# A graph layer with top-16 attention: two broadcasts, the output's products and the gates of the gathers are placed anew in a hand-written order

## The chip, the cores and the metric

One NeuronCore of one Trainium2 chip. The metric is the time of one execution in device microseconds.

## The reference

12500 nodes with 128 features, 200000 edges sorted by their target node. Cut to what matters:

```
h = relu(layernorm(x))
Qv = h @ W_Q.T ; Ku = h @ W_K.T
score = sum(Qv[dst] * Ku[src]) / sqrt(128) * exp(-edge_weight)
keep = the 16 highest scores of each dst
alpha = softmax of the kept scores within each dst
agg = segment_sum(alpha * (h[src] @ W_msg.T), dst)
out = x + relu(h @ W_self.T + agg)
```

## The kernel before

A beginning normalizes all rows of x into a table in memory (`h_tab`) and prepares the edges' tables; it takes the first 200 us or so. The rest is a software pipeline over 112 groups (`G`) of edges. A group is 14 chunks (`GC`) of 128 edges, and a fifteenth chunk (`NJ`) that overlaps the next group, so that every group holds whole nodes, at most 128 of them. Edges lie on the partitions, one chunk to a column.

One iteration of the loop over `i` is a pass. It works on several groups at once, each at another stage: `at(i - 3, sums, 0, 4)` runs the stage `sums` for group i − 3, if there is such a group. The order of the calls is the order on every engine: the schedule is manual, each engine runs its instructions in that order, and only semaphores join the engines.

The stages of a group g, by the pass in which they run:

- `h_turned`, `q_made`, `q_out` (passes g − 2 and g − 1): transpose the nodes' rows (TensorE), copy them out (`hT`), and multiply with the joint query and key weights, to `q`.
- `far_of(g, b)` and `to_edges(g, b)`, b from 0 to 3 (pass g − 1): TensorE copies the row of the edges' distances to the group's first node (`rel`) to all partitions, one bf16 product of up to 512 columns for four chunks (L223, a<-rel,ident), into one of two banks tagged "a". VectorE compares that with the partition's number (L631): `to_e`, a one-hot matrix from nodes to edges.
- `places(g)` (pass g − 1): VectorE builds the one-hot matrices of each edge's slot and of its node in a window (`opo`, L639 and L641).
- `q_to_edges(g, b)` (pass g): four fp32 products that give every edge its node's q, into one of two banks "q".
- `scores(g, b)` (pass g): VectorE multiplies the gathered source rows, the decay and q and sums along the row, once per chunk (L663). `scores_in_slots` spreads the scores over 40 slots (L671, L672).
- `slots_by_node`, `slots_out`, `node_by_slots` (pass g + 1): products that bring the scores of a node into one row.
- `best_begun`, `best`, `sum_of_exps`, `one_over_sum` (pass g + 2): the best 16 and their softmax.
- `kept_to_edges` (pass g + 2): 15 small bf16 products that bring each node's kept slots back to its edges, into bank "x" (L223, x<-km,to_e); `on_edges` (L732 to L739) and `exps` turn them into weights.
- `weights` (L747, L748), `sums`, `sums_out` (pass g + 3): one-hot matrices with weights, and 15 fp32 products that sum the gathered rows by node into bank "e"; ScalarE copies the sums out, divided by the softmax's sum (`agn`, L762).
- `sums_turned`, `sums_turned_out`, `products` (pass g + 4): transpose, copy (`aggT`, L769), and two fp32 products with the self and message weights.
- `output`, `store` (pass g + 5): relu and sum with x (L777), and the store.

One bank of PSUM, `so`, serves four of these: columns 0 to 127 the transposed rows, 128 to 255 the query product, 256 to 383 the transposed sums, 384 to 511 the output's products. VectorE's `output` reads it at the start of a pass, and `sums_turned` writes it right after.

The source rows come by an indirect DMA for each chunk, issued by GpSimd (L183), 14 in a pass, into one of 8 buffers, four to five groups ahead of their use. `gather_behind` makes each wait for the latest TensorE product issued before it in the order; `more(j)`, called 14 times in a pass, is such a gate. `PACED` is 12: until then the gathers run up to a third of a pass further ahead. `rows_asked`, `act_rows` and `rows_named` belong to other queues for single rows, whose rates (`SP_ROWS`, `ACT_ROWS`) are 0.

Of the kernel before, what the change touches and what calls it, by code (L numbers as in the profile page):

```python
# [19 lines left out]
ACT = mybir.EngineType.Activation  # L20

SP_ROWS = 0
ACT_ROWS = 0
PSUM = bass.MemoryType.PSUM

P = 128
# [57 lines left out]
def gnn_layer(  # L84
# [34 lines left out]
    G = -(-CH // GC)  # L119
# [20 lines left out]
    def bank(tag, bufs):  # L140
        return psum.tile([P, 512], F32, tag=tag, bufs=bufs, name=tag)
# [52 lines left out]
    for name, (_, _, p0, rate, j) in STREAMS.items():  # L194
        m = 0
        while rate:
            ready = p0 + (P * m + P - 1) // rate + 1
            g = max(ready, RAW)
# [29 lines left out]
    def gather_behind(g, j):  # L228

        if j < own[g] and (g, j) not in slow:  # L230
            d = gather(g, j, j + 1, lambda j: idx_all[:, GC * g + j:GC * g + j + 1])
            tc.add_manual_dep(d.ins, pe["last"].ins.name, SYNC, reason="behind a product")
# [41 lines left out]
    def raw_stats(g):  # L274
        T[g]["raw"] = row_stats(rows_pool, T[g]["hs"], own[g], f"r{g % 2}")
# [8 lines left out]
    def raw_finished(g, part):  # L284
        rows, (rs, sm) = T[g]["hs"], T[g]["raw"]
        if part < 3:
            normed(rows, 1 + 3 * part, 4 + 3 * part, rs, sm)
            return
        for t in range(10, own[g]):
            nc.vector.tensor_scalar(rows[:, t, :], rows[:, t, :], rs[:, t:t + 1], sm[:, t:t + 1],  # L290
                                    op0=OP.mult, op1=OP.add)
            nc.vector.tensor_scalar(rows[:, t, :], rows[:, t, :], 0.0, None, op0=OP.max)
# [18 lines left out]
    with tc.tile_pool(name="edges", bufs=1) as ep, ExitStack() as stage:  # L311
# [123 lines left out]
        pb = bank("s", 1)  # L435
# [79 lines left out]


    def all_checked():
        pb = bank("a", 2)
        nc.tensor.matmul(pb[0:1, 0:4], lhsT=ones, rhs=badc, start=True, stop=True)
        total = rows_pool.tile([1, 1], F32, name="total")  # L520
        nc.vector.tensor_reduce(total, pb[0:1, 0:4], axis=AX.X, op=OP.add)
        nc.vector.tensor_scalar(any_i, total, 1.0, None, op0=OP.min)
        nc.vector.tensor_scalar(uns, pb[0:1, 1:2], 1.0, None, op0=OP.min)
# [35 lines left out]
    with tc.tile_pool(name="win", bufs=2) as win:  # L559

        so = bank("s", 1)
# [29 lines left out]
        def load_x(g):  # L591
            k = G - TAIL
            if g == k:
                starts(g, 1, TAIL, XT)
            T[g]["x_t"] = rows_pool.tile([P, D], F32, name="x_t", bufs=8)
            if g < k:
                nc.sync.dma_start(T[g]["x_t"], x[ds(T[g]["start", 0], P), :])
            else:
                nc.sync.dma_start(T[g]["x_t"], x_end[ds(T[g]["start", 1], P), :])
# [193 lines left out]
        ready = {name: [] for name in STREAMS}  # L793
        unnamed = {name: [r for i in range(-3, G) for r in rows_at.get((name, i), [])] for name in STREAMS}

        def rows_named(name):

            todo = unnamed[name]
            g, j, e = todo[0]
            n = min(AT_ONCE, P - e)  # L800
            _, numbers = nc.values_load_multi_w_load_instructions(
                late_b[g:g + 1, j - GC + 2, e:e + n], engines=[STREAMS[name][1]], min_val=0, max_val=ROW * (N - 1),
                skip_runtime_bounds_check_because="nodes' numbers times a row's bytes")
            ready[name] += [(g, j, e + k, st) for k, st in enumerate(numbers)]
            del todo[:n]

        def rows_asked(name, most=1000):
            for g, j, e, st in ready[name][:most]:
                m = slow[g, j][1]
                if e == 0:  # L810
                    T[g]["late", j] = win.tile([P, D], F32, name=f"late{name}", bufs=NLATE)
                d = STREAMS[name][0].dma_start(T[g]["late", j][e:e + 1, :].bitcast(U8), h_bytes[ds(st, ROW)])
                d.then_inc(landed[name][m % NLATE], 16)
                tc.no_tile_sem_insts.add(d.ins.name)
                tc.add_to_no_dep_group(f"rows{g}_{j}", d.ins)
            del ready[name][:most]

        def act_rows(i, n):
            if i >= STREAMS["ACT"][2]:
                rows_asked("ACT", n)  # L820
# [6 lines left out]
        def at(g, stage, *args):  # L827
            if 0 <= g < G:
                stage(g, *args)


        for i in range(-3, G - 1):
            at(i + 3, load_nodes)
            due = len(rows_at.get(("SP", i), []))
            first = min(due, len(ready["SP"]))
            rows_asked("SP", first)
            at(i - 1, load_x)
            due -= first
            while due:
                rows_named("SP")  # L840
                n = min(due, len(ready["SP"]))
                rows_asked("SP", n)
                due -= n
            if i == G - 2:
                load_x(G - 2)
                load_x(G - 1)
            if i == 8:
                nc.sync.dma_start(h_tab[N:N + P, :], zpad)
                nc.sync.dma_start(x_end[XT:XT + P, :], zpad)
                nc.sync.dma_start(x_end[0:XT, :], x[N - XT:N, :])  # L850
            def raw(part):
                if i in (1, 2):
                    raw_finished(i + 1, part)

            def more(j):

                if i in (-1, 0, 1):
                    g = i + 6
                elif i < PACED:
                    g, j = (i + 4, j + 4) if j < 10 else (i + 5, j - 10)  # L860
                    if g < 8:
                        return
                else:
                    g = i + 4
                    if i == PACED and j < 4:
                        return
                if i >= -1 and g < G:
                    gather_behind(g, j)

            at(i, q_to_edges, 0)  # L870
            more(0)
            at(i - 5, output)
            at(i - 5, store)
            at(i - 4, sums_turned)
            at(i + 1, far_of, 0)
            at(i - 3, weights)
            at(i - 2, best_begun)
            at(i + 1, far_of, 1)
            more(1)
            at(i - 4, sums_turned_out)  # L880
            at(i + 1, q_out)
            act_rows(i, 3)
            at(i, q_to_edges, 1)
            more(2)
            raw(0)
            at(i + 1, to_edges, 0)
            at(i - 2, best)
            at(i - 2, sum_of_exps)
            act_rows(i, 4)
            for b in range(3):  # L890
                at(i - 1, slots_by_node, b)
            more(3)
            at(i + 1, to_edges, 1)
            at(i - 1, slots_out)
            at(i, scores, 0)
            raw(1)
            at(i + 1, far_of, 2)
            at(i + 1, far_of, 3)
            more(4)
            at(i, q_to_edges, 2)  # L900
            more(5)
            raw(2)
            at(i + 2, h_turned)
            at(i + 2, h_turned_out)
            at(i + 1, to_edges, 2)
            at(i, scores, 1)
            act_rows(i, 3)
            at(i - 2, kept_to_edges)
            more(6)
            at(i - 1, node_by_slots)  # L910
            at(i - 3, sums, 0, 4)
            more(7)
            at(i + 1, to_edges, 3)
            at(i - 3, sums, 4, 7)
            act_rows(i, 3)
            more(8)
            at(i, q_to_edges, 3)
            more(9)
            at(i - 2, one_over_sum)
            act_rows(i, 3)  # L920
            at(i - 3, sums, 7, 11)
            more(10)
            at(i - 3, sums, 11, NJ)
            more(11)
            at(i, scores, 2)
            at(i - 2, on_edges)
            at(i - 3, sums_out)
            at(i - 4, products)
            more(12)
            at(i - 2, exps)  # L930
            at(i + 1, places)
            if len(ready["ACT"]) < ACT_ROWS and unnamed["ACT"] and i >= 2:
                rows_named("ACT")
            act_rows(i, 4)
            at(i, scores, 3)
            at(i, scores_in_slots)
            if i == 0:
                raw_stats(2)
                raw_stats(3)
                raw_begun(2)  # L940
                raw_begun(3)
            if i in (1, 2):
                raw_finished(i + 1, 3)
            at(i + 2, q_made)
            more(13)
            if i > 0 and later:
                later.pop(0)()

# [95 lines left out]
    with tc.tile_pool(name="gen", bufs=1) as gen, tc.If(nc.values_load(  # L1044
# [31 lines left out]
        pb = bank("s", 1)  # L1076
# [142 lines left out]
```

## Time and profile before

| what | value |
|---|---|
| median of 3 runs | 2464.83 us (2458.7 to 2468.15) |
| the profiled execution | 2461.79 us, span 2460.0 us |
| TensorE matmuls, busy | 1633.1 us (66%), 13352 instructions |
| TensorE weight loads, busy | 1420.3 us (58%) |
| VectorE busy | 1668.7 us (68%), 7054 instructions |
| GpSimd busy | 1484.4 us (60%), of it gathers 1421.1 us in 1507 |
| ScalarE busy | 277.0 us (11%) |
| granted TensorE clock, mean | 0.806 |

In the rows of the order of time the first number is the start in us from the span's start, the second the length, then engine, line, operation, what is written and read, and in brackets the idle time of the engine before it and what ended that. "remote" is a release that the profile cannot name. A matmul's record shows when it was begun, and its end is modelled; one fp32 product of 128 by 128 is two records. L223 and L226 are the helpers that issue all products and transpositions of the loop, so there the tiles' names tell the stages apart.

### The profile page before, as it was taken

The page shows a single profiled execution, that of the slowest core. Times are in us where ns is not written, and L with a number is a line of the kernel's source. Part 1 is how long each engine was busy: PE and PEld are TensorE (multiplying, and loading weights), DVE is VectorE, ACT ScalarE, POOL GpSimd, SP SyncE. Part 2 cuts the span into 40 slices and gives each one's busy share as a digit, 9 for nine tenths or more (in the row PEclk, how much of TensorE's full clock was granted, in tenths as well). Part 3 has the DMA queues.
Part 4 walks back from the last instruction along what each step waited for, and adds up shares of the span by engine and source line. Part 5 has one row for each costly group of instructions (what it writes and reads, how often), then busy time and mean ns, then how long its engine had stood idle before and what let it go on. Part 6 is the DMA issues. An engine that isn't in the chain of part 4 may idle for free. (4 is left out here: it accounts for less than half of the span.)

```text
span 2460.0 us, 41443 instructions
## 1 busy us (share of the span) xinstructions
PE 1633.1 (66%) x13352; PEld 1420.3 (58%) x13353; DVE 1668.7 (68%) x7054; ACT 277.0 (11%) x1075; POOL 1484.4 (60%) x1579
## 2 busy tenths in 40 slices
PE   0337777766676676677676766767676767767676
PEld 0236666656565566666666655656565656656566
DVE  5557667666666666667666666666666666667676
ACT  5420000000000000001000000000000000001011
POOL 6653666666666666666666666666666666666640
PEclk9957788778777888787778788887888787888888
DMA  9311222222222222222222222222222222222210
GB/s 247 91 47 35 65 54 55 54 54 54 54 54 56 54 55 55 54 56 53 53 53 53 55 55 54 56 53 54 56 55 54 54 56 54 56 52 56 52 43 9
DMA packets 101470, 143.43 MB, mean 58 GB/s; under 512 B 31063, under 2 KB 74327, under 8 KB 100480
## 3 DMA queue, kind: packets, MB, share of 16 engines
q0 software_dynamic: 50144, 102.74, 16.5%
q1 hardware_dynamic: 51102, 37.99, 5.6%
q8 instruction: 106, 1.74, 0.3%
q14 instruction: 118, 0.97, 0.1%
HBM read 126.79 MB, written 14.40 MB: 57 GB/s over the span
## 5 line engine op out<-in xcount | busy, mean ns | idle before, releaser
L183 POOL DMA_INDIRECT hs<-h_tab,idx_all x1507 | 1421.1, 943 | 859.8 <-issue 308.0
L223 PEld LDWEIGHTS q<-q,to_e 128*128 128x128 f32 x3348 | 541.6, 238 | 255.2 <-DVE prod L663 201.2
L223 PE MATMUL q<-q,to_e 128*128 128x128 f32 x3348 | 589.5, 329 | 76.0 <-DVE prod L663 57.2
L631 DVE TENSOR_SCALAR to_e<-a,nvec 128x512 f32<-128x512 f32 (+1 forms) x447 | 318.8, 714 | 378.0 <-remote 239.6
L663 DVE SCALAR_TENSOR_TENSOR prod<-hs,dec_all,q 128x128 f32<-128x128 f32 x1674 | 482.5, 343 | 30.9 <-issue 15.9
L223 PE MATMUL e<-hs,alz 128*128 128x128 f32 x3240 | 477.1, 303 | 30.5 <-issue 30.2
L223 PEld LDWEIGHTS e<-hs,alz 128*128 128x128 f32 x3240 | 439.0, 215 | 34.6 <-issue 25.5
L226 PE MATMUL s<-ident,agn 128*128 128x128 f32 x112 | 41.6, 371 | 389.8 <-issue 225.8
L223 PE MATMUL e<-opo,sl 128*41 128x40 f32 x3348 | 233.0, 240 | 93.3 <-issue 93.2
L223 PEld LDWEIGHTS e<-opo,sl 128*41 128x41 f32 x3348 | 204.4, 155 | 127.8 <-issue 115.0
L226 PEld LDWEIGHTS s<-ident,agn 128*128 128x128 f32 x112 | 17.9, 160 | 407.6 <-issue 397.4
L223 PE MATMUL a<-rel,ident 112*128 112x512 bf16 (+1 forms) x447 | 185.3, 479 | 92.6 <-DVE km L709 68.9
L777 DVE SCALAR_TENSOR_TENSOR o<-s,x_t 128x128 f32<-128x128 f32 x112 | 32.6, 291 | 231.4 <-remote 223.4
L641 DVE TENSOR_TENSOR opo<-slots,x 128x1200 f32<-128x1200 f32 x109 | 153.0, 1404 | 3.8
L663 DVE DVE_READ_ACCUMULATOR prod<-hs,dec_all,q 128x1 f32 x1674 | 138.9, 83 | 0.1
L762 ACT ACTIVATE agn<-e,rden 128x128 f32<-128x128 f32 x108 | 39.7, 367 | 840.9 <-PE q L223 580.4
L769 ACT COPY aggT<-s 128x128 f32<-128x128 f32 x112 | 29.7, 265 | 607.6 <-remote 360.0
L748 DVE TENSOR_TENSOR alz<-opo,x 128x600 f32<-128x600 f32 x112 | 87.0, 777 | 3.9
L739 DVE TENSOR_REDUCE kept<-mine 128x15 f32<-128x600 f32 x112 | 86.9, 776 | 3.8
L672 DVE TENSOR_TENSOR sl<-opo,x 128x600 f32<-128x600 f32 x110 | 85.6, 778 | 3.8
L737 DVE TENSOR_TENSOR mine<-x,opo 128x600 f32<-128x600 f32 x112 | 86.5, 772 | 0.0
L223 PEld LDWEIGHTS <-to_e 128*128 128x128 bf16 x1674 | 74.7, 110 | 16.6 <-issue 9.1
(184 smaller groups left out, 1356.0 us busy)
## 6 DMA issues: line engine op xcount, KB each, us to landing
hs<-h_tab,idx_all POOLq DMA_INDIRECT x1507
h_r<-h_tab SPq DMA_DIRECT2D x112, 64.0 KB
x_t<-in_x_dram SPq DMA_DIRECT2D x108, 64.0 KB
out_dram<-o SPq DMA_DIRECT2D x108, 64.0 KB
xg<-in_x_dram SPq DMA_DIRECT2D x2, 1400.0 KB
h_tab<-xg SPq DMA_DIRECT2D x2, 1400.0 KB
xg<-in_x_dram SPq DMA_DIRECT2D x1, 1120.0 KB
h_tab<-xg SPq DMA_DIRECT2D x1, 1120.0 KB
```

What stands on the lines that cost most here:

```text
L183: d = nc.gpsimd.indirect_dma_start(out=T[g]["hs"][:, j, :], out_offset=None, in_=table[0:N, :], in_offset=bass.IndirectOffsetOnAxis(ap=ind ...
L223: pe["last"] = nc.tensor.matmul(*args, **how)
L226: pe["last"] = nc.tensor.transpose(*args)
L631: nc.vector.tensor_scalar(T[g]["to_e"][:, n0:n1], T[g]["pr", b][:, 0:n1 - n0], nvec, None, op0=OP.is_equal)
L641: nc.vector.tensor_tensor(T[g]["opo"], slots.unsqueeze(1).unsqueeze(1).to_broadcast([P, 2, NJ, KM]), at_e.unsqueeze(3).to_broadcast([P, 2, ...
L663: nc.vector.scalar_tensor_tensor(prod, rows_of(g, j), dec_all[:, c:c + 1], T[g]["pq", b][:, (j % 4) * P:(j % 4 + 1) * P], op0=OP.mult, op1 ...
L672: nc.vector.tensor_tensor(sl1[g % 2][:, 0:n, 0:KM], T[g]["po"][:, 0:n, :], bc(s[:, 0:n], KM), op=OP.mult)
L737: nc.vector.tensor_tensor(mine[:, 0:n, :], px[:, 0:n, 0:KM], T[g]["po"][:, 0:n, :], op=OP.mult)
L739: nc.vector.tensor_reduce(kept[:, 0:n], mine[:, 0:n, :], axis=AX.X, op=OP.add)
L748: nc.vector.tensor_tensor(alz[g % 2].rearrange("e (j w) -> e j w", w=WW + STEP)[:, 0:n, 0:WN], T[g]["ow"][:, 0:n, :], bc(kept[:, 0:n], WN) ...
L762: nc.scalar.activation(T[g]["agn"], T[g]["pa"], AF.Copy, scale=T[g]["rden"])
L777: nc.vector.scalar_tensor_tensor(T[g]["o"], so[:, 3 * P:4 * P], 0.0, T[g]["x_t"], op0=OP.max, op1=OP.add)
```

## The change

Two of the four broadcasts of distances (`far_of`, b 0 and 1) move from the start of the pass to the end of the pass before; they are then called for group i + 2. The output's two products (`products`) move from the end of a pass to its middle, behind broadcasts 2 and 3. The kept slots' products (`kept_to_edges`) move ahead of the third block of `q_to_edges`. `sums_out`, `places` and `q_made` come right behind scores block 2, and `on_edges` behind `places`. The 14 gates lie elsewhere between these steps. The gathers of groups 5, 6 and 7 run in passes 0, 1 and 2, where they ran in passes −1, 0 and 1. The calls of the row queue with rate 0 are taken out. The check of the edges' form, which runs once, uses bank `so` where it used a bank "a".

```diff
     def all_checked():
-        pb = bank("a", 2)
+        pb = so[:, 3 * P:4 * P]
...
-                if i in (-1, 0, 1):
-                    g = i + 6
+                if i in (0, 1, 2):
+                    g = i + 5
...
-                if i >= -1 and g < G:
+                if i >= 0 and g < G:
                     gather_behind(g, j)
 
             at(i, q_to_edges, 0)
...
             at(i - 5, output)
             at(i - 5, store)
             at(i - 4, sums_turned)
-            at(i + 1, far_of, 0)
             at(i - 3, weights)
             at(i - 2, best_begun)
-            at(i + 1, far_of, 1)
             more(1)
...
             at(i + 1, far_of, 2)
             at(i + 1, far_of, 3)
             more(4)
-            at(i, q_to_edges, 2)
+            at(i - 4, products)
+            at(i - 2, kept_to_edges)
             more(5)
             raw(2)
+            at(i, q_to_edges, 2)
+            more(6)
             at(i + 2, h_turned)
             at(i + 2, h_turned_out)
             at(i + 1, to_edges, 2)
             at(i, scores, 1)
-            act_rows(i, 3)
-            at(i - 2, kept_to_edges)
-            more(6)
             at(i - 1, node_by_slots)
...
             at(i, scores, 2)
+            at(i - 3, sums_out)
+            at(i + 1, places)
+            at(i + 2, q_made)
+            more(12)
+            at(i + 2, far_of, 0)
+            at(i + 2, far_of, 1)
+            more(13)
             at(i - 2, on_edges)
-            at(i - 3, sums_out)
-            at(i - 4, products)
-            more(12)
             at(i - 2, exps)
-            at(i + 1, places)
...
             at(i, scores, 3)
             at(i, scores_in_slots)
...
-            at(i + 2, q_made)
-            more(13)
```

More of the change, by code (lines that the diff above doesn't have):

```diff
@@ L888, in gnn_layer @@
             at(i - 2, sum_of_exps)
-            act_rows(i, 4)
             for b in range(3):
@@ L906, in gnn_layer @@
             at(i, scores, 1)
-            act_rows(i, 3)
-            at(i - 2, kept_to_edges)
-            more(6)
             at(i - 1, node_by_slots)
@@ L914, in gnn_layer @@
             at(i - 3, sums, 4, 7)
-            act_rows(i, 3)
             more(8)
@@ L919, in gnn_layer @@
             at(i - 2, one_over_sum)
-            act_rows(i, 3)
             at(i - 3, sums, 7, 11)
@@ L925, in gnn_layer @@
             at(i, scores, 2)
+            at(i - 3, sums_out)
[5 more added lines that the diff above has]
+            more(13)
             at(i - 2, on_edges)
-            at(i - 3, sums_out)
-            at(i - 4, products)
-            more(12)
             at(i - 2, exps)
-            at(i + 1, places)
-            if len(ready["ACT"]) < ACT_ROWS and unnamed["ACT"] and i >= 2:
-                rows_named("ACT")
-            act_rows(i, 4)
             at(i, scores, 3)
```

## The prediction

> **What bounds the kernel now.** I read the page first, then the stretches by pass, then the waits, then the order of time around one pass boundary.
>
> ```profile
> span 2460.0 us, 41443 instructions
> PE 1633.1 (66%) x13352; PEld 1420.3 (58%) x13353; DVE 1668.7 (68%) x7054; ACT 277.0 (11%) x1075; POOL 1484.4 (60%) x1579
> PEclk9957788778777888787778788887888787888888
> L183 POOL DMA_INDIRECT hs<-h_tab,idx_all x1507 | 1421.1, 943 | 859.8 <-issue 308.0
> L641 DVE TENSOR_TENSOR opo<-slots,x 128x1200 f32<-128x1200 f32 x109 | 153.0, 1404 | 3.8
> ```
>
> No engine is full: 66, 68 and 60 per cent. So this is a loop that waits, and the question is on what. The comparison of one-hot places (L641) runs once in a pass, so its starts mark the passes. The stretches view gives two steady passes, two passes near the end, and one pass after the start.
>
> ```profile
> 1516.54:1558.23 41.69, 28.07 (x240) 24.22 (x240) 28.45 (x120) 3.66 (x16) 26.42 (x28) 0.84 0.21 55
> 2373.78:2402.73 28.95, 22.80 (x240) 20.26 (x240) 27.99 (x121) 3.44 (x16) 1.88 (x2) 1.00 0.07 20
> 369.80:387.30 17.50, 12.45 (x103) 10.64 (x103) 14.09 (x60) 1.36 (x6) 10.03 (x12) 0.80 0.20 54
> ```
>
> The columns are the length, then busy time and count of PE, weight loads, DVE, ACT and POOL, then the granted clock and the DMA share. Two steady passes take 41.69 us, 20.85 each. At the end the same 240 matmuls and the same DVE work (28.45 against 27.99 us) take 28.95, 14.47 a pass. The only work missing there is POOL's: 2 gathers instead of 28. The third row, a pass with 12 gathers in its stretch, lies between at 17.50. So the instruction order alone doesn't set 20.85: in the order of today DVE runs nearly gapless (14.0 of 14.47) once there are no gathers. What the gathers cost shows in the order of time.
>
> ```profile
> 1536.21 1.95 PE L223 MATMUL e<-hs,alz 128*128 128x128 f32 x16
> 1541.95 0.37 ACT L762 ACTIVATE agn<-e,rden 128x128 f32<-128x128 f32 x1 [8.55 <-remote]
> 2386.59 1.95 PE L223 MATMUL e<-hs,alz 128*128 128x128 f32 x16
> 2388.64 0.37 ACT L762 ACTIVATE agn<-e,rden 128x128 f32<-128x128 f32 x1 [4.57 <-PE e L223]
> ```
>
> These are the last message sums of a pass and ACT's reading of them. At the end of the program ACT starts 0.1 us after the records of the sums end (2388.54). In a steady pass it starts 3.8 us after (1538.16 to 1541.95). PE's results become usable late while gathers run, though PE's records stand in time; the traces do not say why. DVE pays for that lateness wherever it asks for a fresh PE result:
>
> ```profile
> DVE to_e L631 <- remote: 110.1, 29, 6.9
> DVE o L777 <- remote: 108.8, 46, 4.1
> DVE to_e L631 <- PE a L223: 45.9, 49, 2.1
> DVE up L732 <- PE e L223: 18.2, 24, 0.8
> DVE o L777 <- PE q L223: 1.4, 1, 1.4
> ```
>
> This is the list of DVE's waits from 1000 to 2000 us, 48 passes. The output waits (108.8 + 1.4) / 48 = 2.3 us a pass, the distance comparisons (110.1 + 45.9) / 48 = 3.25, the kept slots' reduction 0.4. Together 5.9, almost all of the 20.85 − 14.47 = 6.4. The scores, which read the gathered rows, are not in the list: no gather is late.
>
> **The change, part by part.** Two neighbouring passes, at the places it touches:
>
> ```profile
> 1503.21 0.29 DVE L777 SCALAR_TENSOR_TENSOR o<-s,x_t 128x128 f32<-128x128 f32 x1 [3.34 <-remote]
> 1504.71 0.74 DVE L631 TENSOR_SCALAR to_e<-a,nvec 128x512 f32<-128x512 f32 x1
> 1510.66 0.75 DVE L631 TENSOR_SCALAR to_e<-a,nvec 128x512 f32<-128x512 f32 x1 [2.04 <-remote]
> 1521.19 0.29 DVE L777 SCALAR_TENSOR_TENSOR o<-s,x_t 128x128 f32<-128x128 f32 x1 [1.42 <-remote]
> 1521.63 0.30 PE L226 MATMUL s<-ident,agn 128*128 128x128 f32 x1 [3.14 <-DVE x L747]
> 1521.77 0.60 PE L223 MATMUL a<-rel,ident 112*128 112x512 bf16 x2
> 1526.83 0.75 DVE L631 TENSOR_SCALAR to_e<-a,nvec 128x512 f32<-128x512 f32 x1 [4.06 <-remote]
> 1531.46 0.75 DVE L631 TENSOR_SCALAR to_e<-a,nvec 128x512 f32<-128x512 f32 x1 [0.71 <-PE a L223]
> 1544.84 0.29 DVE L777 SCALAR_TENSOR_TENSOR o<-s,x_t 128x128 f32<-128x128 f32 x1 [3.36 <-remote]
> ```
>
> From one output to the next the first pass takes 17.98 us and the second 23.65.
>
> *Two distance broadcasts a pass ahead.* Nothing is added: two bf16 products of 512 columns (0.60 us at 1521.77) move from behind the transposition to before the next pass's first q products. The wait that goes is that of the first comparison: 0 in the short pass, 4.06 in the long one, 2.0 a pass. What is late next is the third comparison: it needs broadcasts 2 and 3, which stay behind the slot sums in PE's order, and it already waits 2.04 and 0.71. DVE that comes 4.06 earlier finds them as late as now unless PE too is earlier. So of 2.0 between 0 and 2.0 is kept.
>
> *Output's products in mid pass.* Two fp32 products (four records) leave the place between the sums and the output:
>
> ```profile
> 1538.00 0.39 PE L223 MATMUL s<-wselfT,hT 128*128 128x128 f32 x2
> 1538.22 0.39 PE L223 MATMUL s<-wmsgT,aggT 128*128 128x128 f32 x2
> 1538.45 0.39 PE L223 MATMUL s<-a_qk,hT 128*128 128x128 f32 x2
> ```
>
> By their records they are 0.45 us (1538.00 to 1538.45). The output then no longer needs anything from the pass's end, if only the products count: its whole 2.3 us would go. But the query product (a_qk, 1538.45) writes the same bank, and the output came 6.4 us after that record, much later than its own two products need; so I keep a wait for a_qk and count the moved 0.45 us, with 0 and 2.3 as ends. The Trainium skill speaks for the low end: "PSUM — Partial Sum Buffer", section "PSUM bank collisions raise a hardware error", says that engines must be kept apart by bank, not by address. By that rule the output still stands behind the query product and this term is near the 0.45; without it, 2.3.
>
> *PE's own stop at the boundary.* The transposition must wait until the output has read its bank: from 1521.19 to 1521.63, 0.44 us in which PE had nothing left. The two broadcasts now stand before it and cover that. Gain 0 to 0.44.
>
> *Kept slots' broadcasts* (15 bf16 products) now stand before the third block of q products: the 0.4 us that the reduction waits goes. The price: scores block 2 gets its products 15 small products later; DVE has the comparisons and scores block 1 in hand then, so nothing.
>
> *Places before on_edges* on DVE: the same six instructions in another order; the sums' copy on ACT keeps its order too. Nothing. SP's queue is untouched.
>
> *Gates.* Still 14 gathers in a pass, each behind a PE product. Two gathers without a held gate are 1.25 us apart:
>
> ```profile
> 1538.67 0.94 POOL L183 DMA_INDIRECT hs<-h_tab,idx_all  x1 [0.30 <-issue]
> 1539.92 0.94 POOL L183 DMA_INDIRECT hs<-h_tab,idx_all  x1 [0.30 <-issue]
> ```
>
> So POOL alone needs 14 × 1.25 = 17.5 us a pass: no steady pass can be shorter for long. The groups 5 to 7 start one pass later; they are used in passes 5 to 7, nothing. The row queues that are taken out (act_rows) have a rate of 0 and issue nothing.
>
> *Sum.* The ceiling is 20.85 − 17.5 = 3.35 us a pass. Against it stands the size of the cause: from 1 gather a pass (14.47) through 12 (17.50) to 14 (20.85), each of the last two costs 1.7 us, and the change takes no gather away. As long as PE's lateness stays, waits move to the third comparison rather than vanish. I take the parts that don't depend on it: 0.4 (reduction) plus half of the 0.44 at the boundary, 0.65 a pass with the rounding in the change's favour. The gathers run in some 105 passes: 105 × 0.65 = 68 us. The profiled run took 2461.8 us (span 2460.0), so 2394; the median of the runs shown is 3 us higher. Forecast: 2395.
>
> **The rivals.**
>
> *The lateness was only costly because DVE stood right behind it.* Then the 2.0 of the first comparison and the 2.3 of the output go too, and the pass falls towards POOL's 17.5: at half of the 3.35, 105 × 1.7 = 178 us, 2285; in full 2110. For it: the short pass, where the first comparison found its broadcast ready, took 17.98. Against it: the third comparison, and the long pass, where PE's results were late almost throughout. The clock row would help: 240 matmuls took 28.07 us at 0.84 and 22.80 at 1.00. The Trainium skill, "TensorE: Matmul & The Clock Gate", section "HAM oscillation", says that idle stretches halve PE's clock and steady feeding keeps it; here the rows agree in direction, and by that rule a PE that stops less would run faster and this rival gains. Chance 0.22.
>
> *Slower: PE no longer gets its restart.* The short pass begins after PE has delivered everything and stopped; the long one begins while its first q products are still undelivered. Today the stop at the output gives every second pass a fresh start. With two broadcasts and four q products queued ahead of the output, PE never stops there, and every pass would be like the long one: up to 23.65 − 20.85 = 2.8 us a pass, 294 us, 2755. It decides from the point where no pass starts with its transposition delivered at once. Part of the long pass is the very wait for the broadcast that the change removes, so I take 0.5 to 1.5 us a pass: 2515 to 2620. Chance 0.30.
>
> *No change.* The same PE work and the same 14 gathers give the same time, and each removed wait comes back at the third comparison: 2462, within 12 us. Chance 0.10.
>
> **How the numbers follow.** The forecast (0.2 to 1.2 us a pass, 2336 to 2441) has 0.38, so faster by over 0.5% (12 us, about what a measurement here can tell) is 0.38 + 0.22 = 0.60, same 0.10, slower 0.30. The range leaves out about a tenth on each side: down to 2230, the lower half of the first rival, and up to 2540, the mild third of the slower one.
>
> **What would show it.** Right: the output's wait falls to about 1.5 us a pass or less, the first comparison has no wait, the third waits more than today (over 1.4 us mean), and the alternation of 20 and 21.7 us passes is gone or weaker. The bigger gain shows as POOL's gathers 1.25 us apart nearly throughout. The slower rival shows as passes of 22 us and more with the third comparison or the scores waiting for PE. The forecast is wrong if the sums' copy on ACT follows its sums at once although gathers run: then the lateness was a matter of the order.

## The result and the profile after

The changed kernel takes 2445.49 us (median of 4 runs, 2443.03 to 2447.96) against 2464.94 us for the kernel before (4 runs, 2458.7 to 2468.15): a ratio of 0.9924 [0.9902, 0.9946], faster by 19 us where 70 were forecast. The profiled execution took 2447.96 us, its span 2446.1 us; the one of before took 2461.79, so the two profiles below differ by 13.9 us of span.

Every comparison met one of two conditions: in the result above and in the experiments f and j TensorE stops beside GpSimd's gathers, and the kernels with all their gathers take 2442 to 2496 us; in e, g, h, i and k it doesn't, and they take 2003 to 2016 us.

The page of the changed kernel:

```profile
span 2446.1 us, 41241 instructions
PE 1683.4 (69%) x13352; PEld 1453.5 (59%) x13353; DVE 1663.8 (68%) x7054; ACT 268.8 (11%) x1075; POOL 1484.6 (61%) x1579
L183 POOL DMA_INDIRECT hs<-h_tab,idx_all x1507 | 1421.3, 943 | 844.4 <-issue 327.6
L663 DVE SCALAR_TENSOR_TENSOR prod<-hs,dec_all,q 128x128 f32<-128x128 f32 x1674 | 482.6, 342 | 269.7 <-remote 216.1
L631 DVE TENSOR_SCALAR to_e<-a,nvec 128x512 f32<-128x512 f32 (+1 forms) x447 | 317.8, 712 | 375.7 <-PE x L223 330.8
```

Each engine works through as many instructions as before. VectorE's idle time has moved: the scores (L663) wait 269.7 us, where the page of before has 30.9, and the comparisons (L631) wait 375.7 us, as long as before (378.0). The profile names the kept slots' products (x) as what ended that wait, but a comparison reads only the bank that a broadcast wrote; x is merely the product whose record ended shortly before. From 1000 to 2000 us the third comparison starts 3.1 us (median) after the records of its own broadcast end, and in the kernel before 3.0.

The passes begin here at 115 us, sooner than the 200 us given above for the beginning. Where the 13.9 us are is read from three stretches, cut at the one-hot comparisons of the first, the sixth and the fourth-last group. First before, then after:

```profile
115.04:224.20 109.16, 58.68 (x413) 48.93 (x413) 71.32 (x308) 16.28 (x48) 53.16 (x57) 0.67 0.16 41
224.20:2373.77 2149.57, 1497.02 (x12266) 1305.19 (x12266) 1469.32 (x6180) 187.46 (x824) 1355.42 (x1438) 0.80 0.21 55
2373.77:2460.00 86.23, 59.98 (x602) 54.41 (x601) 63.73 (x279) 10.29 (x45) 5.86 (x6) 0.91 0.05 13
```

```profile
114.31:206.58 92.27, 56.95 (x407) 47.51 (x407) 70.11 (x304) 16.10 (x47) 52.05 (x56) 0.72 0.17 48
206.58:2356.21 2149.63, 1545.63 (x12271) 1336.54 (x12270) 1463.80 (x6180) 179.09 (x824) 1356.24 (x1439) 0.81 0.19 55
2356.21:2446.10 89.89, 63.45 (x604) 57.73 (x603) 65.36 (x284) 10.69 (x46) 6.36 (x7) 0.88 0.05 13
```

The 103 passes in the middle take 2149.57 and 2149.63 us: 20.87 a pass in both. Nothing was gained in the steady passes. The first five passes are 16.9 us shorter, the stretch ahead of them 0.7 us, and the end is 3.7 us longer: −0.7 − 16.9 + 0.1 + 3.7 = −13.8. (The place of the comparison in a pass moved a little, so an end may hold a microsecond or two of the other.)

Within the first five passes one stands out, first before, then after:

```profile
115.04:144.05 29.01, 7.11 (x37) 5.60 (x36) 7.52 (x30) 0.27 (x1) 21.41 (x23) 0.66 0.23 58
114.31:125.23 10.92, 7.35 (x42) 6.02 (x41) 7.43 (x30) 1.82 (x3) 7.19 (x8) 0.98 0.26 75
```

The same 30 VectorE instructions take 29.01 us beside 23 of GpSimd's instructions and 10.92 beside 8: the gathers of group 5 no longer run there. In the kernel before, GpSimd's gathers follow each other without a break until 141.91 us in that stretch, and VectorE's third block of scores, whose products' records end at 121.32, starts only at 142.73. The second pass is much the same (25.88 us before, 25.36 after); the third and fourth pay back 1.6 us (17.83, then 19.39) and 1.1 us (16.25, then 17.34).

VectorE's waits from 1000 to 2000 us, 48 passes, show what the new order did to the steady passes:

```profile
DVE to_e L631 <- PE x L223: 153.5, 44, 6.4
DVE prod L663 <- remote: 100.0, 45, 2.4
DVE prod L663 <- PE e L223: 19.4, 43, 0.5
DVE to_e L631 <- remote: 11.7, 2, 7.2
DVE o L777 <- remote: 7.3, 3, 3.9
```

The output's wait fell from 2.3 us a pass to 7.3 / 48 = 0.15. The comparisons wait 153.5 / 48 = 3.2 us a pass, now at the third one only, and the scores, which did not wait before, wait (100.0 + 19.4) / 48 = 2.5: the first of these rows is nearly all block 0, the second block 2. The five rows make 6.1 us a pass; the five rows of before made 5.9. One pass in the order of time, at the places the prediction followed:

```profile
1504.47 0.28 DVE L777 SCALAR_TENSOR_TENSOR o<-s,x_t 128x128 f32<-128x128 f32 x1
1504.90 0.30 PE L226 MATMUL s<-ident,agn 128*128 128x128 f32 x1 [1.94 <-DVE sl L672]
1506.04 0.74 DVE L631 TENSOR_SCALAR to_e<-a,nvec 128x512 f32<-128x512 f32 x1
1511.18 0.35 DVE L663 SCALAR_TENSOR_TENSOR prod<-hs,dec_all,q 128x128 f32<-128x128 f32 x1 [2.30 <-remote]
1515.75 0.75 DVE L631 TENSOR_SCALAR to_e<-a,nvec 128x512 f32<-128x512 f32 x1 [3.41 <-PE x L223]
1521.60 0.62 PE L223 MATMUL e<-hs,alz 128*128 128x128 f32 x4 [0.94 <-issue]
1524.18 0.37 ACT L762 ACTIVATE agn<-e,rden 128x128 f32<-128x128 f32 x1 [3.73 <-PE q L223]
1525.31 0.28 DVE L777 SCALAR_TENSOR_TENSOR o<-s,x_t 128x128 f32<-128x128 f32 x1
```

Output (1504.47) and first comparison (1506.04) start without a wait; scores block 0 waits 2.30 us, the third comparison 3.41. ACT's copy of the sums still starts 1.96 us after the records of the sums end (1522.22 to 1524.18). Over all steady passes that lag is 1.8 us (median), and in the kernel before 2.2; the 3.8 us of the prediction's pass is at its long end. The alternation is gone: most passes are 20.8 to 20.9 us, with 14 gathers each. In the kernel before, the passes of 20.0 us have 13 gathers begun in them and those of 21.8 us have 15; which of the two, length or number, follows from the other is not shown.

### The profile page after: what moved, and what is told of

It reads as the page before. It is cut to its first block, busy times and chain, and to the rows that moved or that the text cites. A ratio compares the mean times of both kernels' runs of the same rounds, so it can differ in the third digit from the quotient of the medians.

```text
span 2446.1 us, 41241 instructions
## 1 busy us (share of the span) xinstructions
PE 1683.4 (69%) x13352; PEld 1453.5 (59%) x13353; DVE 1663.8 (68%) x7054; ACT 268.8 (11%) x1075; POOL 1484.6 (61%) x1579
## 3 DMA queue, kind: packets, MB, share of 16 engines
q0 software_dynamic: 50144, 102.74, 14.8%
## 5 line engine op out<-in xcount | busy, mean ns | idle before, releaser
L663 DVE SCALAR_TENSOR_TENSOR prod<-hs,dec_all,q 128x128 f32<-128x128 f32 x1674 | 482.6, 342 | 269.7 <-remote 216.1
L223 PE MATMUL q<-q,to_e 128*128 128x128 f32 x3348 | 571.3, 315 | 50.8 <-issue 40.0
L631 DVE TENSOR_SCALAR to_e<-a,nvec 128x512 f32<-128x512 f32 (+1 forms) x447 | 317.8, 712 | 375.7 <-PE x L223 330.8
L223 PEld LDWEIGHTS q<-q,to_e 128*128 128x128 f32 x3348 | 512.0, 224 | 91.0 <-issue 61.2
L223 PE MATMUL e<-opo,sl 128*41 128x40 f32 x3348 | 271.6, 238 | 314.6 <-issue 314.2
L223 PEld LDWEIGHTS e<-opo,sl 128*41 128x41 f32 x3348 | 220.7, 151 | 374.6 <-issue 369.6
L223 PE MATMUL a<-rel,ident 112*128 112x512 bf16 (+1 forms) x447 | 169.0, 467 | 13.0 <-DVE to_e L631 10.8
L226 PE MATMUL s<-ident,agn 128*128 128x128 f32 x112 | 35.1, 313 | 189.3 <-DVE sl L672 144.8
L663 DVE DVE_READ_ACCUMULATOR prod<-hs,dec_all,q 128x1 f32 x1674 | 136.9, 82 | 0.0
L223 PEld LDWEIGHTS <-to_e 128*128 128x128 bf16 x1674 | 90.4, 118 | 38.5 <-issue 27.8
L223 PE MATMUL x<-km,to_e 128*128 128x43 bf16 x1674 | 94.9, 208 | 25.6 <-issue 22.5
L223 PEld LDWEIGHTS s<-wselfT,hT 128*128 128x128 f32 x224 | 69.5, 322 | 33.5 <-issue 30.0
```

Source lines behind the costliest of these rows:

```text
L223: pe["last"] = nc.tensor.matmul(*args, **how)
L226: pe["last"] = nc.tensor.transpose(*args)
L631: nc.vector.tensor_scalar(T[g]["to_e"][:, n0:n1], T[g]["pr", b][:, 0:n1 - n0], nvec, None, op0=OP.is_equal)
L663: nc.vector.scalar_tensor_tensor(prod, rows_of(g, j), dec_all[:, c:c + 1], T[g]["pq", b][:, (j % 4) * P:(j % 4 + 1) * P], op0=OP.mult, op1 ...
```

## Experiments

Two questions were put. Where do the 19 us come from: the gathers' later start, or the new order? And what sets the 20.87 us of a steady pass: GpSimd, held up at its gates (theory C), or a cost on TensorE for each gather, whenever it runs (theory D)? Four kernels recur.

"Start pace only" is the kernel before with

```diff
-                if i in (-1, 0, 1):
-                    g = i + 6
+                if i in (0, 1, 2):
+                    g = i + 5
...
-                if i >= -1 and g < G:
+                if i >= 0 and g < G:
```

"Old start pace" is the kernel after with these lines undone. "No gates" is the kernel after without one line:

```diff
-            tc.add_manual_dep(d.ins, pe["last"].ins.name, SYNC, reason="behind a product")
```

"Half the gathers" is the kernel after with 7 gathers in a pass from group 20 on; an odd chunk there computes with the rows of its even neighbour:

```diff
+        if g >= 20 and j % 2:
+            return
...
+            if g >= 20 and j < GC:
+                j -= j % 2
```

**First comparison (e).** Expected:

> The kernel before, with only the first three gated groups of gathers (5, 6, 7) moved from passes -1, 0, 1 to passes 0, 1, 2. Theory A (all of the change's gain is made at the start, because the first passes issue 14 gathers fewer; the steady pass stays 20.85 us): 2440 to 2450 us, about 15 to 19 us faster than before. Theory B (the gain comes from the new order of the steady passes, spread over them, 0.18 us each): within 4 us of before.

> The kernel after, with groups 5, 6, 7 gathered in passes -1, 0, 1 again as before. Theory A (the gain is made at the start): 2460 to 2468 us, no faster than before. Theory B (the gain comes from the new order): 2445 to 2450 us as after.

> The kernel after without the 14 gates: each gather of the loop goes as soon as its buffer is free. Theory C (GpSimd is held up by gates that open late, 14 times 1.25 us plus 3.3 us of held gates): the pass falls towards 17.5 us, about 2100 to 2200 us. Theory D (every gather costs TensorE a stretch of time, so TensorE's results are late whatever the order, and 14 gathers make the pass): the pass stays at 20.8 us within 0.5, 2400 to 2500 us.

> The kernel after with every second gather of a group left out from group 20 on (7 in a pass; the chunks without rows of their own use the neighbour's). Theory D (a price of about 0.8 us for each gather on TensorE): the pass falls to about 15 us, close to VectorE's 14.4. Theory E (something else than the gathers sets 20.8 us, the end of the program is short only because its passes have other work): the pass stays near 20 us.

Measured, against a kernel before at 2009.3 us: start pace only 2009.68, ratio 1.0 [0.9991, 1.0009]; old start pace 2006.54, 0.9987 [0.9978, 0.9996]; no gates 2007.09, 0.9985 [0.9975, 0.9994]; half the gathers 1737.06, one run. The kernel before itself is some 455 us faster here than in the first result, which the expectations had not foreseen; they were written for the first result's condition, and this comparison decides neither between A and B nor between C and D. The stretches of "start pace only" and its waits from 1000 to 1900 us say what bounds it there:

```profile
199.84:228.50 28.66, 22.64 (x240) 20.11 (x240) 27.80 (x120) 3.44 (x16) 21.65 (x24) 1.00 0.35 91
1158.62:1193.57 34.95, 25.84 (x238) 22.86 (x238) 28.55 (x120) 3.88 (x16) 26.41 (x29) 0.90 0.24 65
DVE prod L663 <- DMA hs<-h_tab,idx_all: 118.2, 130, 2.2
```

Two early passes take 14.33 us each with VectorE nearly gapless (27.80 of 28.66), and two later ones 17.48 with GpSimd's gathers end to end, 14 × 1.249; VectorE then waits for gathered rows. The lead of four to five groups is eaten by about pass 25. So here the kernel is bound by GpSimd at the floor of 17.5 us that the prediction gave, and order, gates and start have almost nothing to move; the new order is worth 0.1 to 0.2% of it. Half the gathers takes GpSimd out, and from group 20 on two passes take 28.74 us, 14.37 each:

```profile
1029.42:1058.16 28.74, 22.88 (x242) 20.56 (x241) 27.84 (x121) 3.44 (x16) 13.41 (x15) 1.00 0.18 47
```

The sums' copy on ACT, which in the first profile of before started 3.8 us late, follows at once in this same order of steps:

```profile
1171.34 1.95 PE L223 MATMUL e<-hs,alz 128*128 128x128 f32 x16
1173.38 0.37 ACT L762 ACTIVATE agn<-e,rden 128x128 f32<-128x128 f32 x1 [4.56 <-PE e L223]
```

The records end at 1173.29, the copy starts at 1173.38, and gathers began at 1170.93 and 1172.18. Gathers alone do not make TensorE late, then.

**Plain loads (f).** The kernel after once more, and a version in which from group 20 on each gather is a load of 128 neighbouring rows, so of as many bytes, behind the same gate; the sums then take those rows and not the edges' own:

```diff
-            d = gather(g, j, j + 1, lambda j: idx_all[:, GC * g + j:GC * g + j + 1])
+            if g < 20:
+                d = gather(g, j, j + 1, lambda j: idx_all[:, GC * g + j:GC * g + j + 1])
+            else:
+                if j == 0:
+                    T[g]["hs"] = rows_pool.tile([P, GC, D], F32, name="hs", bufs=8)
+                d = nc.sync.dma_start(T[g]["hs"][:, j, :], h_tab[P * j:P * (j + 1), :])
```

> The changed kernel itself, beside the kernel before on the same chip. Theory F (the runs of the first result met a TensorE that stood still in steps of 0.7 us; without these stops both kernels are bound by GpSimd's 14 gathers of 1.25 us): both about 2008 us, within 4 us of each other, and no steps of 0.7 us in TensorE's records. Theory G (the kernels differ by what the first result showed, wherever they run): 0.992 of the kernel before.

> The kernel after with the gathers of groups from 20 on replaced by plain loads of 128 neighbouring rows on SP's queue, as many and as large, behind the same gates (the rows are the wrong ones). If GpSimd's issue is the bound (theory F), the pass falls from 17.5 us to VectorE's 14.35, about 1740 us. If the traffic of the gathered rows is, it stays at 17.5 us, about 2008 us.

Measured: the kernel after 2444.17 against 2462.04, ratio 0.9925 [0.9908, 0.9942], the first result again, as theory G had it; with plain loads 1839.19 (one run), more than the 1740 of the expectation because the passes that still gather take 20.8 us here. Within that one execution the steady pass goes from 20.85 us to 14.35, over the one pass in which the loads replace the gathers (the middle row, with 7 gathers begun in it):

```profile
242.91:284.50 41.59, 29.62 (x223) 25.57 (x222) 28.39 (x120) 3.47 (x16) 26.40 (x29) 0.76 0.26 70
426.69:444.16 17.47, 11.60 (x102) 9.42 (x101) 14.25 (x60) 2.00 (x9) 7.12 (x8) 0.90 0.23 60
1133.37:1162.07 28.70, 22.84 (x242) 20.52 (x241) 27.81 (x120) 3.46 (x16) 0.00 (x0) 1.00 0.28 80
```

The last row has the order, the gates and the bytes (80 GB/s, more than the first), and no GpSimd work. So the 6.5 us of a pass belong to the gathers as GpSimd issues them, not to the order, the gates or the amount of traffic. (The packets do differ: 4096 bytes in the gathers, 512 in the loads, and the loads take the same rows for every group.) Theories C and D would both have it so.

**The four kernels again (g), and single ones (h, i).**

> The kernel before with only the start pace of the change (groups 5, 6, 7 gathered in passes 0, 1, 2). If the chip shows the 0.7 us stops (kernel before near 2462 us): theory A (the gain is made at the start) 2443 to 2450 us; theory B (the gain comes from the new order) within 4 us of before. If it doesn't (before near 2009 us): same as before.

> The kernel after with the start pace of before. With the stops: theory A 2458 to 2468 us, theory B 2440 to 2448 us. Without: 2006 us.

> The kernel after without the 14 gates. With the stops: if the gates hold GpSimd up (theory C), 2100 to 2250 us; if each gather costs TensorE time (theory D), the pass stays 20.8 us, 2420 to 2480 us. Without the stops: 2006 us.

> The kernel after with every second gather left out from group 20 on (7 in a pass). With the stops: theory D (TensorE pays for each gather, about 0.7 to 0.8 us) 14.4 to 16 us a pass, 1860 to 2000 us; if the stops come by time rather than by gather, near 20 us a pass, 2300 us or more. Without the stops: 1737 us.

> The kernel before with only the start pace of the change. On a chip where TensorE shows stops of 0.7 us beside the gathers (kernel before near 2462 us): theory A (the gain of the change is made in passes 0 and 1) 2443 to 2450 us; theory B (it comes from the new order) 2458 to 2466 us. On a chip without the stops (before near 2010 us): equal to before.

> The kernel after without the 14 gates. On a chip with the stops: theory C (the gates hold GpSimd up) 2100 to 2250 us; theory D (TensorE pays for each gather, gate or not) 2420 to 2480 us, with passes of 20.8 us. On a chip without the stops: 2007 to 2010 us.

> The kernel before with only the start pace of the change. On a chip where TensorE stops for 0.7 us at a time beside the gathers (kernel before near 2462 us): theory A (the gain of the change is made in passes 0 and 1) 2443 to 2450 us; theory B (it comes from the new order) 2458 to 2466 us. On a chip without the stops: equal to before.

> The kernel after with every second gather left out from group 20 on. On a chip with the stops: theory D (TensorE pays 0.7 to 0.8 us for each gather) 14.4 to 16 us a pass; if the stops come by time and not by gather, near 20 us a pass. On a chip without the stops: 14.35 us a pass, about 1738 us.

None of these showed the stops. g, against 2012.42 and in the order of the expectations: 2013.0, ratio 1.0003 [0.9994, 1.0013]; 2009.93, 0.9989 [0.998, 0.9999]; 2009.69, 0.9987 [0.9978, 0.9997]; 1740.39 (one run). h, against 2009.57: start pace only 2008.93, ratio 0.9997 [0.9987, 1.0006], and no gates 2009.92 (one run). i, against 2009.53: start pace only 2009.65, ratio 1.0001 [0.9992, 1.0011], and half the gathers 1739.0 (one run). The reading is that of e again: start pace 0.0%, order 0.1%.

**The decisive pair (j).**

> The changed kernel beside the kernel before. On a chip where TensorE stops beside the gathers (kernel before near 2462 us): 0.992 again, 2443 to 2447 us. On a chip without the stops (before near 2010 us): 0.998 to 1.000, since GpSimd's 14 gathers of 1.25 us bound both (17.5 us a pass) and the start pace gains nothing there.

> The kernel before with only the start pace of the change, on the same chip. With the stops: theory A (the gain is made in passes 0 and 1) 2443 to 2450 us; theory B (it comes from the new order) 2458 to 2466 us. Without: equal to before.

Here the stops were there. The kernel before takes 2494.87 us, the kernel after 2478.32, ratio 0.9936 [0.992, 0.9953], and the start pace alone 2482.83, 0.995 [0.9934, 0.9967]. In absolute times both expectations missed, by 31 to 40 us, because the kernel before stands at 2495 and not at 2462; against it the start pace gains 12 us, the lower end of theory A's 12 to 19. Of 16.6 us, 12 come with the start pace; the intervals overlap, so the split is rough by the times, but the stretches agree with it. First the kernel after, then start pace only:

```profile
113.28:206.70 93.42, 55.73 (x409) 46.54 (x409) 70.28 (x304) 16.37 (x48) 52.69 (x56) 0.74 0.18 48
206.70:2389.28 2182.58, 1556.64 (x12270) 1335.93 (x12268) 1468.66 (x6180) 178.70 (x823) 1359.61 (x1438) 0.81 0.21 54
2389.28:2477.10 87.82, 60.59 (x604) 54.69 (x603) 65.29 (x284) 10.69 (x46) 6.32 (x7) 0.91 0.05 13
```

```profile
115.31:211.93 96.62, 60.11 (x416) 50.23 (x416) 71.81 (x309) 16.13 (x48) 53.19 (x57) 0.70 0.18 47
211.93:2394.77 2182.84, 1506.89 (x12263) 1309.24 (x12262) 1468.20 (x6180) 187.21 (x824) 1355.41 (x1438) 0.80 0.21 54
```

The old order and the new one take 2182.84 and 2182.58 us for the 103 middle passes. The new order is worth 2.0 us ahead of the first comparison and 3.2 us in the first five passes, less 1.0 at the end (87.82 against 2481.6 − 2394.77 = 86.8), and nothing in between. Two orders that wait at different places thus take the same time to 0.3 us, here as in the first result, though the level is 33 us higher here: what sets the steady pass is something that neither order touches.

**No gates, once more (k).**

> The changed kernel, one look, as the companion of the next run on the same chip. If TensorE's stops beside the gathers are there (the kernel before at 2460 to 2495 us in this comparison), 2440 to 2480 us with even passes of 20.8 us; if they aren't, 2005 to 2012 us with passes of 17.5 us.

> The changed kernel with no gather waiting for a gate. If the kernel before is at 2460 to 2495 us here: theory C (GpSimd, held up at gates, sets the 20.8 us of a pass) expects gathers back to back, passes of 18 to 19 us and 2100 to 2250 us; theory D (each gather costs TensorE time, whenever it runs) expects the mean pass to stay at 20.5 to 21.5 us while gathers run, 2420 to 2500 us. If the kernel before is at 2010 us, both expect 2005 to 2015 us and nothing is told apart.

The stops were absent: 2009.23 and 2010.43 us beside 2010.67 for the kernel before, one run each. The times don't tell C and D apart. They do show the kernel after itself in both conditions, so it is not the changed kernel that brings the stops.

**What the traces add, and what stays open.** Theory C can be judged without the missing run. In the loop GpSimd only gathers, so it can hold the others up only with rows that come late. By the times of their packets, the rows of each group from 20 to 107 have landed at least 60 us, about three passes, before the group's first score starts, in the profiles of both kernels with stops. In k1, without them, the last rows land 9.6 us (median) after that start. So with stops a GpSimd that is held up at gates is not what a pass waits for. For theory D speaks the pass of 17.47 us in f: 7 gathers cost it 3.1 us over the 14.35, and 14 cost 6.5, about 0.45 us each. That is one pass; the kernels without gates and with half the gathers never met the stops.

How a gather stops TensorE isn't known, and the stops aren't TensorE's alone. In the second pass of the changed kernel VectorE takes the statistics (L240) of raw rows that were gathered some 40 us earlier, and VectorE and TensorE go on in the same steps of 0.7 us or twice that; in k1 the same 14 instructions run without a gap (last row):

```profile
133.91 0.20 PE L223 MATMUL e<-opo,sl 128*41 128x40 f32 x1 [1.88 <-issue]
134.58 0.29 DVE L240 BATCH_NORM_STATS2 str<-hs 128x6 f32<-128x128 f32 x1 [0.21 <-issue]
135.29 0.29 DVE L240 BATCH_NORM_STATS2 str<-hs 128x6 f32<-128x128 f32 x1 [0.42 <-issue]
135.31 0.23 PE L223 MATMUL e<-opo,sl 128*41 128x40 f32 x1 [1.20 <-issue]
135.99 0.29 DVE L240 BATCH_NORM_STATS2 str<-hs 128x6 f32<-128x128 f32 x1 [0.41 <-issue]
113.21 2.79 DVE L240 BATCH_NORM_STATS2 str<-hs 128x6 f32<-128x128 f32 x14
```

Steps of 0.6 to 0.8 us from the start of one record of a matmul or weight load to the next number 231 in the first profile of before, 489 in that of the changed kernel, and 12 in e1. Their number doesn't measure the loss, since the first two kernels have equal passes. The gathers' packets took no longer (16.5% of 2460 us before, 14.8% of 2446 after, 20.1% of 2006 in e1).

The recording differs too. The trace of the changed kernel holds 12777 semaphore updates with stops and 39310 in k1; in f2 ten passes with gathers have 224 of VectorE's 410 updates, and ten passes with loads have all 410. So in the profiles with stops a name like "remote" or "x" for what ended a wait is often a guess. Whether the gathers stop the engines and the recording alike, or the recording itself holds the engines up, no run here tells apart. Nor is it known why the stops are there in one comparison and not in another: e, i and j ran on one and the same chip.

## Why the prediction was right and wrong

The sign was right and the range (2230 to 2540) held the time, but the gain came from elsewhere than it said, from a term that stood at nothing: the right sign was luck.

*The step that failed: 0.65 us a pass kept, 105 passes, 68 us.* Measured 0.00: 2149.57 against 2149.63. The reduction's 0.4 us did go from where it stood: the list of VectorE's waits has no row for it any more. As much now stands at scores block 2, whose later products were priced at "nothing": VectorE waits 19.4 / 48 = 0.4 us a pass for them. PE's stop at the output was mis-sized. It was read as the 0.44 us from the output's start to the transposition, but that row has 3.14 us of idle time before it, and over 48 passes PE stands idle 181.4 us, 3.8 a pass, before the transposition. In the changed kernel that is 82.2 us, 1.7 a pass, and it is still the output that it waits for: in both kernels 108 of 111 transpositions start 0.15 us after the output ends, whatever name the list gives (`sl`, x). The 2.1 us saved there came back inside PE's other work, as stops at the products of bank "e" for which no release is seen. PE's waits from 1000 to 2000 us, first before, then after:

```profile
PE s L226 <- issue: 98.2, 23, 6.1
PE s L226 <- DVE o L777: 51.5, 16, 4.4
PE e L223 <- issue: 46.5, 68, 1.2
```

```profile
PE e L223 <- issue: 164.5, 205, 1.9
PE s L226 <- DVE sl L672: 61.2, 36, 3.1
PE s L226 <- DVE x L747: 7.0, 4, 2.8
```

The row for "e" grows from 46.5 / 48 = 1.0 to 164.5 / 48 = 3.4 us a pass. VectorE, too, stands idle as long as before: 322.2 us in these 48 passes, 316.3 before. Scores block 0, which no term of the prediction mentions, waits 100.0 / 48 = 2.1 us a pass.

*The other step that failed: groups 5 to 7 start one pass later, "nothing".* It was costed by when the rows are used. It should have been costed by what runs beside the gathers in the pass they leave: 29.01 us became 10.92, and with what was paid back the start pace alone is 12 us of the 16.6 in j. The prediction had the rule for it in its own text, that a gather costs the pass it runs in, and used it only for the steady passes.

*Right: waits move to the third comparison rather than vanish.* It said over 1.4 us mean; it is 3.2. *Right: the first comparison has no wait, the output's falls below 1.5 us, the alternation goes.* All three were put down as signs of the forecast, and all three came without any gain: they are signs that the order works as written, not that time is saved.

*The output's wait,* 2.3 us, was taken to stay in part because the query product writes the same bank. It fell to 0.15. In the kernel before VectorE reached the output 3.0 us after the query product's record and waited 3.36 us more (1538.45, 1541.48, 1544.84); now it comes 3.2 us after that record (1501.25, 1504.47) and doesn't wait. But before, the output's own two products lay within half a microsecond of the query product (1538.00 to 1538.45), so which of them the output waited for is not shown. The rule of the Trainium skill ("PSUM — Partial Sum Buffer", "PSUM bank collisions raise a hardware error"), by which the output must stay behind that product, is neither borne out nor refuted: no run here shows the output ahead of it.

*The rivals.* "No change" described the steady passes exactly and missed the start. The slower one, a PE without its restart at 23.65 us a pass, did not come: even passes of 20.84. "Lateness only costly because VectorE stood right behind it" fell in the first profile, where the output and the first comparison wait no more and the waits reappear at the scores and the third comparison. Its ceiling, GpSimd's 17.5 us, is real: the passes of e, g, h, i and k with all their gathers run at it.

*One inference of the prediction holds only with the stops, and at another size.* From passes of 14.47, 17.50 and 20.85 us it read a price of 1.7 us for each of the last two gathers. With the stops the pass with 7 gathers in f took 17.47, so the average price is about 0.45; from 11 gathers (18.1 us in the changed kernel) to 14 it is 0.9. Without the stops the same order takes 14.3 us with 12 gathers and 17.5 with 14, and there it is GpSimd's own issue that counts. The prediction's test (the sums' copy follows at once although gathers run) came true in e1; but what had gone was not an effect of the order, since e1 has the old one.

*The clock.* The granted clock went from 0.806 to 0.814, too little to time anything by. "TensorE: Matmul & The Clock Gate", section "HAM oscillation", of the Trainium skill ties idle stretches to a slower clock; the trace agrees in direction (0.76 in f's passes with gathers, 1.00 in those without), but these passes differ in their waits too, so no gain was shown to come from the clock.

## What to carry over

A wait that leaves the list is a gain only if the distance from pass to pass shrinks: put the sum of the waits and the length of the stretch beside each other before and after, since here 5.9 us of waits became 6.1 at other instructions, and the passes stayed at 20.87. Cost a moved transfer by the pass it leaves as well as by the pass that uses it, the start of the pipeline above all, where a pass can be full of transfers and nearly empty of work. And run the kernel before in every comparison: an effect that holds in one condition of the machine (12 us for the start pace) was 0.0% in the other.

## What was not expected of the hardware

The same kernel took 2465 and 2495 us in some comparisons and 2009 in others, a fifth less, with the same instructions. The runs of 2442 us and more show TensorE going on in steps of about 0.7 us, once VectorE in the same steps, and results that reach their readers 2 to 4 us after the records end, only in passes with GpSimd's gathers; with plain loads of the same size in their place a pass takes 14.35 us, as short as the steady passes at the end of the program. In the same passes the recording misses many semaphore updates, so it may have a part in it; that stays open. Free of that, a gather of 128 rows of 512 bytes costs GpSimd 0.94 us and 0.30 to the next, 1.25 us from start to start, for 1550 of them in e1.
